# The order of one DMA queue: rows, factors and tiles issued ahead of transfers that wait

## The chip, the cores and the metric

The kernel runs on one core of a Trainium2 chip. The metric is the device time of one execution in microseconds; before the change it is 4508.77 us (median of three runs, 4507.54 to 4514.38). TensorE (PE) multiplies, VectorE (DVE) and ScalarE (ACT) work on elements, and SyncE (SP) issues nearly all DMA transfers, in order, from one queue.

## The reference

Two layers over a batch of 8 entries, N = 2048 nodes, D = 256 channels, H = 8 heads of 32. Cut to what matters:

```python
# layer 0, a graph attention layer; prior is adj too
x_proj = einsum('bnd,hdf->bhnf', x, W)
e = leaky_relu(e_src[..., :, None] + e_dst[..., None, :], 0.2)
e = e + softplus(beta) * log(prior + 1e-6)
attn = softmax(where(adj > 0, e, lowest), axis=-1)
x = layernorm(x + (attn @ x_proj) @ W_out.T)
# layer 1, dot-product attention on the same graph
e = leaky_relu((x @ W1) @ (x @ W2).T, 0.2)
attention = softmax(where(adj > 0, e, -1e12), axis=-1)
x = layernorm(x + relu(attention @ (x @ W3)))
```

Both layers are dense 2048 x 2048 per entry, layer 0 for each of 8 heads.

## The kernel before, in words

Everything is float32. Layer 0 never forms the exponentials of e: with m = the mask times the prior to the power beta, it takes s = max(c, r) * m^T on tiles of 128 source nodes by 2048 target nodes, where c is a row of target factors (the same in all partitions) and r a column of source factors. That is one VectorE instruction (L368), one for each head and tile. The sources' own factor is folded into v (the projected x) and into a column e; both factors come in a small tile `re`, and v in a tile of 2 MB.

A **unit** of layer 0 is a pair of heads `hp` (NP = 4) and a tile `jt` of sources (NT = 16), so 64 units make an entry. `Gat.step` does one: it takes the next m^T tile from `self.mts`, makes two s (L368), loads the next m^T (`mt`, 1 MB, from `mt_d` in HBM), and on TensorE multiplies s with v into `val` and with e into `den` (L403), each product 16 instructions in four column groups. For some jt, listed in `SUMMED`, the den product is left out and s is summed instead in a **chain**: the first jt by ScalarE (`d`, L385), the others by VectorE (L379), and one product with ones at the end of the pair. There are four s tiles (two units), two m^T tiles (tag `mt`), two `d` tiles, three c tiles, and three tiles of tag `ht` that several things share: den's copy `dn`, the reciprocals in rows `rb`, x groups `xg` and the queries h1.

At the end of a pair `finish` copies val and den out, and then works in pieces, one per later unit: it brings den's four rows into a tile of 128 partitions (`rc`, four transfers), takes the reciprocal, stores it in `rec_d`, and, every second pair, loads it back with each row repeated over 32 partitions (`rb`, eight transfers of 128 KB) and multiplies the heads with it (L437).

Layer 1 of an entry (`Dot`) runs beside layer 0 of the next. `Dot.step` does 128 target rows: transposes of p and products with h3 into `acc` (L545, L561), the next rows' scores (`e`, L524; the mask `pen` is loaded here), and z = relu(acc/den) + x1 row (L568, L569; the row is `x1r`, loaded at L566), a layer norm and the store. `fill(k)` puts units of the next entry's layer 0 in three places of the step. Between two entries, at the **turn**, `Gat.output` makes layer 0's end (`y`, L463, with x in groups `xg`), `Gat.turn` the transposes and h3, and `Gat.load` fetches the next entry's v and re.

The projections of all entries, and all of entry 0's layer 0, come first; those of entry 1 stay in SBUF, the others go through `v_d` and `re_d`. TensorE's order is the program's own throughout. From L642 on SyncE's is too: a transfer that waits for its tile holds up everything behind it. Elsewhere, and on VectorE and ScalarE, a scheduler fixes the order when the program is built, from priorities in the program's order and a model of the times.

Of the kernel before, what the change touches and what calls it, by code (L numbers as in the profile page):

```python
# [9 lines left out]
F32 = mybir.dt.float32  # L10
# [8 lines left out]
P = 128  # L19
# [8 lines left out]
def kernel(  # L28
# [26 lines left out]
    nc = tc.nc  # L55
    B, N, D = x.shape
    H, _, DH = w_proj.shape
    NT = N // P
# [3 lines left out]
    HALF = N // 2  # L62
    HP = 2
    NP = H // HP
    IG = BK // P


    SUMMED = [[()] * NP, [(2, 4, 5)] + [(1, 4, 7, 10, 13)] * (NP - 1)]
    SUMMED += [[(2, 4, 5)] + [(1, 3, 5, 7, 9, 11, 13)] * (NP - 1)] * (B - 2)

    const = ctx.enter_context(tc.tile_pool(name="const", bufs=1))
    dram = ctx.enter_context(tc.tile_pool(name="dram", bufs=1, space=DRAM))
# [86 lines left out]
    c_d = dram.tile([B, H, N], F32, name="c_d")  # L159
    v_d = dram.tile([B, P, NT, D], F32, name="v_d")  # L160
    re_d = dram.tile([B, P, 2, NT, H], F32, name="re_d")
    rec_d = dram.tile([B, NP, 4, HALF], F32, name="rec_d")
    x1_d = dram.tile([B, N, D], F32, name="x1_d")

    def load_x(b, g):
# [34 lines left out]
    def load_mt(jt, deep):  # L200
        mt = wide_tile("mt", "d" if deep and jt % 2 else "mt", 2)
        nc.sync.dma_start(mt, mt_d[ts(jt, P), :])
        return mt
# [26 lines left out]
    def row_tile(name, bufs=4):  # L230
        return small.tile([P, D], F32, tag="row", name=name, bufs=bufs)


    class Gat:
# [73 lines left out]
        def load(self):  # L308
            self.v = whole.tile([P, NT, D], F32, name="v")
            nc.sync.dma_start(self.v, v_d[self.b])  # L310
            self.re = small.tile([P, 2, NT, H], F32, name="re", bufs=3)
            nc.sync.dma_start(self.re, re_d[self.b])

# [6 lines left out]
        def load_ahead(self):  # L320


            self.mt_loads = (load_mt(jt, False) for _ in range(self.b, B) for _ in range(NP) for jt in range(NT))
            self.c_loads = (gats[b].query_rows(h) for b in range(self.b, B) for h in range(H))
            self.mts, self.cs_ahead = [], []
            for _ in range(2):
                self.cs_ahead.append(next(self.c_loads))
                self.mts.append(next(self.mt_loads))
            self.cs_ahead.append(next(self.c_loads))

        def follow(self, gat):

# [10 lines left out]
        def step(self, count=1):  # L343

            for _ in range(count):
                hp, jt = next(self.units)
                for work in list(self.later):
                    if next(work, self) is self:
                        self.later.remove(work)
                if jt == 0:  # L350
                    if self.b > 0:
                        self.cs = [self.cs_ahead.pop(0) for _ in range(HP)]
                    else:
                        self.cs = [self.query_rows(hp * HP + a) for a in range(HP)]
                    self.val = pacc.tile([P, HALF], F32, tag="val", name="val")
                    self.den = pacc.tile([P, HALF], F32, tag="den", name="den")
                first = self.b == 0 and hp == 0
                if first:
                    self.more_mt(jt + 2, jt > 0)
                if self.b > 0:  # L360
                    mt = self.mts.pop(0)
                else:
                    mt = self.mts[jt] if first else load_mt(jt, True)
                s = []
                for a in range(HP):
                    h = hp * HP + a
                    sa = wide_tile("s", "s", 4)
                    nc.vector.scalar_tensor_tensor(sa, self.cs[a], self.re[:, 0, jt, h:h + 1], mt, ALU.max, ALU.mult)  # L368
                    s.append(sa)
                    if self.b > 0 and jt == NT - 1:  # L370
                        self.cs_ahead += [c for c in [next(self.c_loads, None)] if c]
                if self.b > 0:
                    self.mts += [t for t in [next(self.mt_loads, None)] if t]
                v, e = self.v, self.re[:, 1]
                heads = [hp * HP + a for a in range(HP)]
                chain = SUMMED[self.b][hp]
                if jt - 1 in chain[1:]:
                    for d, sa, h in zip(self.sums, self.last, heads):
                        nc.vector.scalar_tensor_tensor(d, sa, e[:, jt - 1, h:h + 1], d, ALU.mult, ALU.add)  # L379
                self.last = s  # L380
                self.products(self.val, [v[:, jt, ts(h, DH)] for h in heads], s, jt == 0, jt == NT - 1)
                if jt in chain[:1]:
                    self.sums = [wide_tile("d", "d", 2) for _ in heads]
                    for d, sa, h in zip(self.sums, s, heads):
                        nc.scalar.activation(d, sa, AF.Copy, scale=e[:, jt, h:h + 1])  # L385
                if jt not in chain:
                    self.products(self.den, [e[:, jt, h:h + 1].to_broadcast([P, DH]) for h in heads], s, jt == 0,
                                  not chain and jt == NT - 1)
                if chain and jt == NT - 1:
                    self.products(self.den, [ones] * HP, self.sums, False, True)  # L390
                if jt == NT - 1:
                    work = self.finish(hp)
                    next(work)
                    if self.b == 0:
                        for _ in work:
                            pass
                    else:
                        self.later.append(work)
# [8 lines left out]
        def finish(self, hp):  # L407

            b, lo = self.b, hp % 2 * HP * DH
            if hp == 0:
                self.ht = whole.tile([P, NT, KC, P], F32, tag="heads", name="ht")
            ht = self.ht[:, :, hp // 2, :]
            for s in range(2):
                nc.scalar.copy(ht[lo:lo + HP * DH, ts(s, NT // 2), :],
                               self.val[ts(s, HP * DH), :].rearrange("p (t i) -> p t i", i=P))
            dn = chunk.tile([P, HALF], F32, tag="ht", name="dn", bufs=3)
            nc.scalar.copy(dn, self.den)
            yield  # L420
            yield
            rc = small.tile([P, HALF // DH], F32, name="rc", bufs=1)
            for q in range(4):
                nc.sync.dma_start(rc[ts(q, DH), :], dn[q * DH:q * DH + 1, :])
            nc.vector.reciprocal(rc, rc)
            yield
            nc.sync.dma_start(rec_d[b, hp].rearrange("q (p c) -> (q p) c", c=HALF // DH), rc)
            if lo == 0:
                return
            yield  # L430
            for s in range(2):
                rb = chunk.tile([P, HALF], F32, tag="ht", name="rb", bufs=3)
                for a in range(2 * HP):
                    nc.sync.dma_start(rb[ts(a, DH), :], rec_d[b, hp - 1 + a // HP, s * HP + a % HP:s * HP + a % HP + 1, :]
                                      .to_broadcast([DH, HALF]))
                half = ht[:, ts(s, NT // 2), :]
                nc.vector.tensor_mul(half, half, rb.rearrange("p (t i) -> p t i", i=P))  # L437

# [61 lines left out]
    class Dot:  # L500
# [34 lines left out]
        def step(self, fill=lambda k: None):  # L535


            it, (p, den) = self.at, self.ahead
            self.at += 1
            fill(0)  # L540

            def turned(g):
# [19 lines left out]
            fill(2)  # L562
            rec = small.tile([P, 1], F32, name="rec1", bufs=2)
            nc.vector.reciprocal(rec, den)
            xr = row_tile("x1r")
            nc.sync.dma_start(xr, x1_d[self.b, ts(it, P), :])  # L566
            z = row_tile("z")
            nc.scalar.activation(z, acc, AF.Relu, scale=rec)  # L568
            nc.vector.tensor_add(z, z, xr)  # L569
# [61 lines left out]
    count = (B - 1) * NT  # L631
    for k in range(1, NP * NT + 1):
        g0.step()
        if k % 2 == 0:
            for _ in range(k * count // (NP * NT) - (k - 2) * count // (NP * NT)):
                next(projections)
            if k > NT:
                next(weights, None)
# [5 lines left out]
    for b in range(1, B + 1):  # L644
        gat, fresh = gats[b - 1], gats[b] if b < B else None

        def layer_0(count):
            if fresh:
                fresh.step(count)

        if b == 1:
            fresh.load_ahead()
        elif fresh:
            fresh.load()
            fresh.follow(gat)
        rows, turns = gat.output(), gat.turn()
        if dot is None:
            layer_0(4)
            next(rows)
            next(projections)  # L660
            layer_0(2)
        else:

            dot.step(lambda k: layer_0((0, 2, 2)[k]))
            if not fresh:
                for work in gat.later:
                    for _ in work:
                        pass
            next(rows)
            dot.step(lambda k: layer_0((0, 2, 0)[k]))  # L670

        for g in range(NB + 2):
            if g < NB:
# [43 lines left out]
```

## Time and profile before

| | |
|---|---|
| time, median of three runs | 4508.77 us |
| span of the profiled execution | 4502.4 us |
| TensorE, VectorE, ScalarE busy | 4279.3, 3604.1, 1661.5 us |
| mean granted TensorE clock | 0.980 |
| HBM traffic | 185 GB/s over the span |
| m^T loads | 496 of 1024 KB, median 4.9 us to landing |
| x1r loads | 128 of 128 KB, median 4.8 us to landing |
| rb loads | 128 of 128 KB, median 5.5 us to landing |

In the profile a line such as "L368 DVE" names the kernel's line and the engine. Behind a group stands its busy time, the mean of one in ns, and the engine's idle time just before it with what ended it. In a timeline the columns are start, duration, engine, line, operation, out<-in, count, and in brackets the idle time before it and who ended it. A transfer in SyncE's queue is shown when it is issued, after its waits; when it lands isn't in the row.

### The profile page before, as it was taken

How to read it: one execution, taken by the hardware profiler on the slowest of the kernel's cores; microseconds unless marked ns; L12 is line 12 of the kernel's file. 1: busy time of each engine (PE TensorE's matmuls, PEld its weight loads, DVE VectorE, ACT ScalarE, POOL GpSimd, SP SyncE). 2: the span in 40 equal slices, each digit the busy share in tenths (PEclk: the TensorE clock that was granted, in tenths of full speed). 3: DMA queues.
4: the chain of work that ended last, by engine and by line, in shares of the span. 5: the costliest groups of instructions: out<-in, count | busy, mean ns of one | idle time of the engine just before them, and what ended most of it. 6: DMA issues, size and time to landing. Idle time of an engine off the chain costs nothing.

```text
span 4502.4 us, 59957 instructions
## 1 busy us (share of the span) xinstructions
PE 4279.3 (95%) x25040; PEld 2217.8 (49%) x25040; DVE 3604.1 (80%) x2610; ACT 1661.5 (37%) x3021; POOL 9.5 (0%) x14
## 2 busy tenths in 40 slices
PE   7999799998999999998999989999999989999999
PEld 4444255454544445544455545444454544544666
DVE  6888778887798878888789977988798887899222
ACT  6522133332333323332333323333333323433455
POOL 0000000000000000000000000000000000000000
PEclk9999899999999999999999999999999999999999
DMA  8877555656455564555555464555645455554211
GB/s 255 291 266 264 204 204 212 217 194 228 169 188 184 191 216 144 189 184 196 188 188 181 164 215 167 188 187 188 210 147 195 178 202 186 183 183 143 74 50 40
DMA packets 251984, 839.12 MB, mean 186 GB/s; under 512 B 33344, under 2 KB 151872, under 8 KB 176448
## 3 DMA queue, kind: packets, MB, share of 16 engines
q1 hardware_dynamic: 216384, 801.72, 50.4%
q10 hardware_dynamic: 35328, 33.56, 2.2%
q8 instruction: 196, 3.21, 0.3%
q14 instruction: 76, 0.62, 0.0%
HBM read 761.53 MB, written 73.14 MB: 185 GB/s over the span
## 4 chain that ended last, share of the span: by engine, by line
PE 49%; DVE 23%; issue 11%; DMA 6%; ACT 3%; SPq 0%; DVEq 0%; POOL 0%; ACTq 0%; POOLq 0%
DVE s L368 14%; PE acc L561 13%; PE e L524 11%; PE val L403 11%; PE den L403 6%; DVE d L379 4%; PE pt L545 3%; DMA mt<-mt_d 3%; DVE p L529 3%; PE h3p L494 2%; DMA re<-re_d 1%; PE h1p L514 1%; ACT p L532 1%; PE y L463 1%; DMA adj_r<-in_adj_dram 1%
## 5 line engine op out<-in xcount | busy, mean ns | idle before, releaser
L368 DVE SCALAR_TENSOR_TENSOR s<-c,re,mt 128x2048 f32<-128x2048 f32 x1024 | 2362.7, 2341 | 300.6 <-PE den L403 161.7
L403 PE MATMUL val<-s,v 128*32 128x512 f32 x8192 | 1069.2, 611 | 136.4 <-DVE s L368 136.2
L561 PE MATMUL acc<-h,pts 128*128 128x256 f32 x4096 | 956.4, 381 | 18.9 <-ACT pts L547 18.9
L524 PE MATMUL e<-x1t,h 128*128 128x512 f32 x2048 | 904.8, 594 | 2.5 <-ACT h L516 2.5
L561 PEld LDWEIGHTS acc<-h,pts 128*128 128x128 f32 x4096 | 748.7, 191 | 117.2 <-ACT pts L547 30.7
L403 PE MATMUL den<-s,re 128*32 128x512 f32 x5600 | 709.6, 596 | 0.1
L547 ACT COPY pts<-pt 128x512 f32<-128x512 f32 x512 | 296.4, 582 | 942.4 <-PE pt L545 942.1
L403 PEld LDWEIGHTS val<-s,v 128*32 128x32 f32 x8192 | 247.2, 111 | 786.0 <-issue 516.1
L379 DVE SCALAR_TENSOR_TENSOR d<-s,re,d 128x2048 f32<-128x2048 f32 x268 | 622.8, 2342 | 0.0
L524 PEld LDWEIGHTS e<-x1t,h 128*128 128x128 f32 x2048 | 379.0, 190 | 454.0 <-issue 414.8
L529 DVE CUSTOM_DVE_ANT_0 p<-p,pen 128x2048 f32<-128x2048 f32 x128 | 292.4, 2284 | 229.7 <-ACT p L526 229.4
L526 ACT ACTIVATE p<-e 128x512 f32<-128x512 f32 x512 | 303.9, 594 | 422.8 <-PE e L524 420.9
L403 PEld LDWEIGHTS den<-s,re 128*32 128x32 f32 x5600 | 192.2, 111 | 429.9 <-issue 424.1
L545 PEld LDWEIGHTS pt<-ident,p 128*128 128x128 f32 x2048 | 239.6, 141 | 229.3 <-issue 178.2
L532 ACT ACTIVATE p<-p,neg 128x2048 f32<-128x2048 f32 x128 | 256.7, 2006 | 212.6 <-DVE neg L529 212.6
L545 PE MATMUL pt<-ident,p 128*128 128x128 f32 x2048 | 320.8, 280 | 5.2 <-ACT p L532 5.2
L569 DVE TENSOR_TENSOR z<-z,x1r 128x256 f32<-128x256 f32 x128 | 53.8, 420 | 205.9 <-ACT z L568 97.8
L568 ACT ACTIVATE z<-acc,rec 128x256 f32<-128x256 f32 x128 | 61.0, 476 | 284.5 <-PE acc L561 230.0
L270 PE MATMUL proj<-wp,xt 128*128 128x272 f32 (+1 forms) x512 | 134.1, 404 | 15.0 <-ACT both L274 11.1
L494 PE MATMUL h3p<-w3s,x1t 128*128 128x256 f32 x512 | 125.0, 388 | 14.9 <-ACT x1t L489 13.9
L385 ACT ACTIVATE d<-s,re 128x2048 f32<-128x2048 f32 x56 | 111.9, 2009 | 63.9 <-DVE s L368 63.9
L270 PEld LDWEIGHTS proj<-wp,xt 128*128 128x128 f32 x512 | 93.4, 193 | 56.6 <-issue 21.0
(89 smaller groups left out, 1892.6 us busy)
## 6 DMA issues: line engine op xcount, KB each, us to landing
mt<-mt_d SPq DMA_DIRECT2D x496, 1024.0 KB, 4.9
c<-c_d SPq DMA_DIRECT2D x64, 1024.0 KB, 5.5
pen<-pen_d SPq DMA_DIRECT2D x112, 512.0 KB, 5.6
xg<-in_x_dram SPq DMA_DIRECT2D x60, 512.0 KB, 5.0
adj_t<-in_adj_dram SPq DMA_DIRECT2D x16, 1024.0 KB, 8.1
mt_d<-mt SPq DMA_DIRECT2D x16, 1024.0 KB, 5.7
rb<-rec_d SPq DMA_DIRECT2D x128, 128.0 KB, 5.5
x_d<-ht ACTq DMA_DIRECT2D x32, 512.0 KB, 4.3
```

The source lines that it names most:

```text
L270: nc.tensor.matmul(t[:, 0:cols], xt[:, kc, ts(it % IG, P)], wp[:, kc, 0:cols], start=(kc == 0), stop=(kc == KC - 1))
L368: nc.vector.scalar_tensor_tensor(sa, self.cs[a], self.re[:, 0, jt, h:h + 1], mt, ALU.max, ALU.mult)
L379: nc.vector.scalar_tensor_tensor(d, sa, e[:, jt - 1, h:h + 1], d, ALU.mult, ALU.add)
L403: nc.tensor.matmul(dst[ts(q, DH), ts(c, BK)], weights[q % 2], s[q % 2][:, ds(q // 2 * HALF + c * BK, BK)], start=start, stop=stop)
L494: nc.tensor.matmul(t[:, ts(i, D)], x1t[:, kc, ts(2 * (j - 1) + i, P)], w3s[:, kc, :], start=(kc == 0), stop=(kc == KC - 1))
L524: nc.tensor.matmul(t, self.h1[:, kc, ts(it % IG, P)], self.x1t[:, kc, ts(c, BK)], start=(kc == 0), stop=(kc == KC - 1))
L526: nc.scalar.activation(p[:, ts(c, BK)], t, AF.Prelu, alpha=ALPHA)
L529: nc.vector.tensor_tensor_reduce(p, p, pen, -1.0, FMAX, ALU.add, ALU.min, neg)
L532: nc.scalar.activation(p, p, AF.Exp, bias=neg, scale=-1.0, accum_out=den)
L545: nc.tensor.transpose(t[:, ts(k, P)], p[:, ts(g * IG + k, P)], ident)
L547: nc.scalar.copy(pt, t)
L561: nc.tensor.matmul(acc, now[:, ts(k, P)], self.h3[:, j, :], start=(j == 0), stop=(j == NT - 1))
```

## The change

It reorders what SyncE issues, and joins and drops some work around that:

- x1r is loaded at the head of `Dot.step`, not at its end, behind the units' transfers.
- re of the next entry is loaded by `load_factors` at the first unit of the last pair, 16 units before the turn; `load` fetches v alone.
- The first m^T tiles of entry 1 are requested as entry 0's last unit is written, still under the scheduler's order, four instead of two. In entry 1's first pair odd tiles use the two `d` tiles, so four m^T are held; later two again.
- For the `d` tiles to be free, entry 1's first pair has no chain: `()` in place of `(2, 4, 5)`.
- `rc` comes in one transfer instead of four, and each `rb` in one instead of four, from a `rec_d` laid out so that its four rows follow each other.
- At a turn the first x groups (`next(rows)`) are requested behind two units of the second step, not ahead of it.

```diff
-    SUMMED = [[()] * NP, [(2, 4, 5)] + [(1, 4, 7, 10, 13)] * (NP - 1)]
+    SUMMED = [[()] * NP, [()] + [(1, 4, 7, 10, 13)] * (NP - 1)]
...
-    rec_d = dram.tile([B, NP, 4, HALF], F32, name="rec_d")
+    rec_d = dram.tile([B, NP // 2, 2, 2, 2, HALF], F32, name="rec_d")
...
             nc.sync.dma_start(self.v, v_d[self.b])
+
+        def load_factors(self):
             self.re = small.tile([P, 2, NT, H], F32, name="re", bufs=3)
...
-            self.mt_loads = (load_mt(jt, False) for _ in range(self.b, B) for _ in range(NP) for jt in range(NT))
+            self.mt_loads = (load_mt(jt, b == self.b and hp == 0)
+                             for b in range(self.b, B) for hp in range(NP) for jt in range(NT))
...
-            for _ in range(2):
+            for _ in range(3):
                 self.cs_ahead.append(next(self.c_loads))
                 self.mts.append(next(self.mt_loads))
-            self.cs_ahead.append(next(self.c_loads))
+            self.mts.append(next(self.mt_loads))
...
+                if self.b > 0 and hp == NP - 1 and jt == 0 and self.b + 1 < B:
+                    gats[self.b + 1].load_factors()
...
-                if self.b > 0:
+                if self.b > 0 and len(self.mts) < (4 if not SUMMED[self.b][hp] and jt < NT - 4 else 2):
                     self.mts += [t for t in [next(self.mt_loads, None)] if t]
...
-            for q in range(4):
-                nc.sync.dma_start(rc[ts(q, DH), :], dn[q * DH:q * DH + 1, :])
+            nc.sync.dma_start(rc, dn[::DH, :].rearrange("q (p c) -> q p c", c=HALF // DH))
...
-                for a in range(2 * HP):
-                    nc.sync.dma_start(rb[ts(a, DH), :], rec_d[b, hp - 1 + a // HP, s * HP + a % HP:s * HP + a % HP + 1, :]
-                                      .to_broadcast([DH, HALF]))
+                src = rec_d[b, hp // 2, s]
+                nc.sync.dma_start(rb, bass.AP(tensor=src.tensor, offset=src.offset,
+                                              ap=[[HALF, 2 * HP], [0, DH], [1, HALF]]))
...
             it, (p, den) = self.at, self.ahead
             self.at += 1
+            xr = row_tile("x1r")
+            nc.sync.dma_start(xr, x1_d[self.b, ts(it, P), :])
             fill(0)
...
-            xr = row_tile("x1r")
-            nc.sync.dma_start(xr, x1_d[self.b, ts(it, P), :])
...
         g0.step()
+        if k == NP * NT:
+            gats[1].load_ahead()
...
-        if b == 1:
-            fresh.load_ahead()
-        elif fresh:
+        if b > 1 and fresh:
             fresh.load()
...
-            next(rows)
-            dot.step(lambda k: layer_0((0, 2, 0)[k]))
+            def fill(k):
+                if k == 1:
+                    layer_0(2)
+                    next(rows)
+
+            dot.step(fill)
```

More of the change, by code (lines that the diff above doesn't have):

```diff
@@ L422, in finish @@
             rc = small.tile([P, HALF // DH], F32, name="rc", bufs=1)
-            for q in range(4):
-                nc.sync.dma_start(rc[ts(q, DH), :], dn[q * DH:q * DH + 1, :])
+            nc.sync.dma_start(rc, dn[::DH, :].rearrange("q (p c) -> q p c", c=HALF // DH))
             nc.vector.reciprocal(rc, rc)
             yield
-            nc.sync.dma_start(rec_d[b, hp].rearrange("q (p c) -> (q p) c", c=HALF // DH), rc)
+            for s in range(2):
+                nc.sync.dma_start(rec_d[b, hp // 2, s, hp % 2].rearrange("a (p c) -> (a p) c", c=HALF // DH),
+                                  rc[ts(s, HP * DH), :])
             if lo == 0:
```

## The prediction

> **What bounds the kernel now.** I read the page first, then the busy time by stretches, then the timeline of the worst stretch on three engines. The page:
>
> ```profile
> span 4502.4 us, 59957 instructions
> PE 4279.3 (95%) x25040; PEld 2217.8 (49%) x25040; DVE 3604.1 (80%) x2610; ACT 1661.5 (37%) x3021; POOL 9.5 (0%) x14
> ...
> L368 DVE SCALAR_TENSOR_TENSOR s<-c,re,mt 128x2048 f32<-128x2048 f32 x1024 | 2362.7, 2341 | 300.6 <-PE den L403 161.7
> L403 PE MATMUL val<-s,v 128*32 128x512 f32 x8192 | 1069.2, 611 | 136.4 <-DVE s L368 136.2
> ```
>
> TensorE is the bound on average, and of its 223 us of idle time 136 are waits for VectorE's s. Where these lie is told by the busy time of stretches (columns: stretch, length, then each engine's busy time, clock, DMA share, GB/s):
>
> ```profile
> 497.00:570.00 73.00, 46.78 (x266) 14.31 (x259) 61.95 (x51) 9.11 (x16) 0.00 (x0) 0.81 0.61 213
> 1625.00:2064.00 439.00, 434.11 (x2546) 221.79 (x2534) 385.23 (x264) 162.15 (x281) 0.00 (x0) 1.00 0.51 181
> 2064.00:2149.00 85.00, 70.68 (x412) 33.24 (x414) 64.17 (x55) 23.70 (x43) 0.00 (x0) 0.88 0.60 213
> ```
>
> The middle of an entry is full: TensorE idles 4.9 of 439 us, so nothing that speeds other engines there pays. The turn from one entry to the next is not: 14.3 of 85 us idle, and a clock of 0.88. There are six such turns (idle 14.3 to 15.5 us each) and the start of entry 1 (26.2 us). One turn in the timeline, VectorE, TensorE and SyncE's queue (start, duration, instruction, idle before it and who ended it):
>
> ```profile
> 2073.20 0.42 DVE L569 TENSOR_TENSOR z<-z,x1r 128x256 f32<-128x256 f32 x1 [8.81 <-DMA x1r<-x_d]
> ...
> 2078.65 2.35 DVE L368 SCALAR_TENSOR_TENSOR s<-c,re,mt 128x2048 f32<-128x2048 f32 x1 [4.35 <-DMA re<-re_d]
> 2080.92 2.28 DVE L529 CUSTOM_DVE_ANT_0 p<-p,pen 128x2048 f32<-128x2048 f32 x1
> ...
> 2105.64 4.61 DVE L368 SCALAR_TENSOR_TENSOR s<-c,re,mt 128x2048 f32<-128x2048 f32 x2 [4.41 <-PE val L403]
> ```
> ```profile
> 2081.05 1.91 PE L403 MATMUL val<-s,v 128*32 128x512 f32 x2 [3.94 <-DVE s L368]
> 2085.53 2.78 PE L403 MATMUL val<-s,v 128*32 128x512 f32 x11 [2.56 <-DVE s L368]
> ...
> 2119.36 1.92 PE L403 MATMUL val<-s,v 128*32 128x512 f32 x2 [7.14 <-DVE s L368]
> ```
> ```profile
> 2062.02 2.58 SPq L317 DMA_DIRECT2D c<-c_d  x2
> 2064.70 0.38 SPq L202 DMA_DIRECT2D mt<-mt_d  x1
> 2065.12 0.43 SPq L566 DMA_DIRECT2D x1r<-x_d  x1
> 2066.27 0.32 SPq L310 DMA_DIRECT2D v<-v_d  x1
> 2066.64 0.58 SPq L312 DMA_DIRECT2D re<-re_d  x1
> 2067.26 0.44 SPq L209 DMA_DIRECT2D pen<-pen_d  x1
> ```
>
> The reader is to see: the x1 row and the factors re are issued last, behind two c, one m^T and the 2 MB of v. VectorE waits 8.81 us for the row and 4.35 us for the factors, TensorE then waits for s.
>
> Entry 1 starts otherwise: VectorE stands still for 7.99 us until 512.33, waiting for an m^T that SyncE issued at 503.00, behind a 2 MB v_d store (502.14).
>
> [...] SyncE's three xg, which wait for ht tiles, span 13.93 us from 2103.51, and the next m^T goes out at 2117.49, right after the last. [...] 0.50 from 2081 to 2091, with 7.39 us busy, so 3.7 us of work lost.
>
> **The change part by part.**
>
> x1r to the head of the step, re sixteen units early. z needs ScalarE's z too, which ends at 2071.6 (it follows two copies of val and one of den). So z's wait shrinks by only 1.6 us, to 7.2, but with re present VectorE can fill it: m^T and c of the first unit landed by 2066.6, and two of the four s tiles are free then. Static order is the scheduler's, and not known. If two s go ahead of z, VectorE has all four s of units 0 and 1 by 2077.4, then waits for pen (it landed at 2079.82; some 0.4 us earlier without x1r and re in front, still behind v) and does p until 2081.7. TensorE starts val at about 2078 (v, issued at 2066.27, lands some 12 us later) instead of 2081.05, runs units 0 and 1 (4 products of 1.72 us: 6.9) to 2084.9, its transposes and acc (8.4 us, 2095.2 to 2103.6 now) to 2093.3 and the next val to 2095.1, where s tiles come free for unit 4. Now that is 2105.64: 10.5 us earlier, the 3.7 us of half clock included. If the order stays s, p, s, s, s, p still waits for pen until 2079.4 and the gain is 3.5 us. I take 8.5: the first order, less 1 us for semaphores and less 1 us for row sums (below). The 7.14 us before 2119.36 stays: from unit 4's start VectorE needs 13.7 us for two s, two ht products, two d and one s, while TensorE has 2.4 us of work. Six turns: 51 us.
>
> Entry 1: four m^T tiles ahead. m^T 2 and 3 are loaded before the v_d store, as the d tiles are free. The 7.99 us go, and the waits of 0.31 and 2.37 us later: 10.7. Without the chain VectorE drops four d of 2.33 us: 9.3. TensorE gains three den products and drops one against ones, 3 x 1.72 - 1.72 = 3.4 us, beside VectorE, which bounds until 568 (61.95 of 73 us busy against 46.78). TensorE's own work from there, 33.7 us from 506.7, would end at 540.4, before VectorE's 548.5, so VectorE stays the bound and the sum holds: 10.7 + 9.3 = 20.0; the dropped product against ones (1.9 us at 612.4) lies where TensorE is the bound: 1.9. Together about 21.5.
>
> Row sums in single transfers. Four rc issues (2.41 us of SyncE) become one; eight rb (4.99 us) become two. Saved issue time hides nothing now, since SyncE waits for s anyway: 0. On four engines an rb of 512 KB puts 131 KB on each. [...] From above: m^T, 1024 KB, lands in 4.9 us and the fastest x1r, 128 KB, in 2.0, so 896 KB take 2.9 us, 19.3 GB/s per engine, 6.8 us. [...] In the middle of an entry the two ht products come 11.9 and 18.3 us after the first issue (1308.29 to 1320.14 and 1326.59): hidden, but for up to 1 us. In a turn m^T of unit 5 lands behind them, 0 to 1.4 us late: I charge 1.
>
> x groups behind the steps: an m^T now stuck until 2117.49 still lands in time (s of its unit at 2126.7), and the xg, needed at 2137.3, would be issued about 10 us before need with 5 us to land: 0. Waits added for SyncE: x1r's tile was freed two steps earlier and the factors' tile an entry earlier, so nothing is held up. x1r waits in mid-entry (9.2 us of VectorE in 1625 to 2064) go, but TensorE is full there: 0.
>
> Sum: 4508.8 - 51 - 21.5 = 4436.
>
> **Rivals.** (a) The scheduler leaves p in front of s, or pen behind v holds the turn: 6 x 3.5 + 21.5 = 42, so 4466. For it: pen lands 1.1 us before p now. Against: without the wait for re nothing asks for that order. (b) More: the ht products move into the wait before unit 4 and the 7.14 us go too: 6 x 16 + 21.5 = 117, so 4391. Against: their row sums land too late for that. (c) Slower: row sums on four engines become the wait. At 9.2 us later, and 2.9 for m^T behind them, unhidden in six turns (73 us), and 4 us in seven middles (28), 101 is lost against 72.5 gained: 4537. For it: m^T has two tiles only and lands behind. Against: 12 to 18 us of room in the middles.
>
> **How the numbers follow.** Forecast and its neighbourhood (turns worth 6 to 11 us) 0.55, (a) 0.22, (b) 0.12, (c) in full or in part 0.11. The range leaves out half of (b)'s far end and most of (c): 4398 to 4494. Faster by over 0.2% takes the first three, less a little of (a), and the mild part of (c): 0.87; same 0.04; slower 0.09.
>
> **What would show it.** Right: z's wait at a turn is for ScalarE and no longer for x1r; none for re; val after the e products idles about 1 us, not 3.94; clock near 1.00 there; the 7.14 us still present; at entry 1 no 15.20 us gap and some 20 us less to the first h3p. Wrong: VectorE or TensorE waiting for rb, pen or m^T at the turns; rb landing over 15 us after issue and s waiting behind it; TensorE idle in the middles over 10 us.

## The result and the profile after

The changed kernel takes 4540.76 us (median of four runs, 4537.86 to 4541.70) against 4510.67 us for the kernel before, run beside it (four runs, 4507.54 to 4514.38). The ratio is 1.0065, with a 95% interval of 1.0048 to 1.0083: slower by some 30 us, where 73 us of gain had been forecast.

The page of the changed kernel: span, busy time by engine, the chain by line, and four groups (line, engine, operation, tiles, count, then busy time, mean of one in ns, and the engine's idle time ahead of the group with what ended most of it):

```profile
span 4539.9 us, 59623 instructions
...
PE 4289.9 (94%) x25072; PEld 2221.2 (49%) x25072; DVE 3602.1 (79%) x2606; ACT 1660.3 (37%) x3019; POOL 9.5 (0%) x14
...
DVE s L373 13%; PE e L530 12%; PE acc L569 12%; PE val L408 9%; PE den L408 6%; DMA rb<-rec_d 5%; DMA mt<-mt_d 4%; DVE d L384 3%; PE pt L553 3%; PE h1p L520 2%; PE h3p L500 2%; DVE p L535 1%; PE y L469 1%; ACT d L390 1%; ACT p L538 1%
...
L373 DVE SCALAR_TENSOR_TENSOR s<-c,re,mt 128x2048 f32<-128x2048 f32 x1024 | 2354.6, 2342 | 205.7 <-PE den L408 147.1
L408 PE MATMUL val<-s,v 128*32 128x512 f32 x8192 | 1064.0, 613 | 136.6 <-DVE s L373 134.6
...
L575 DVE TENSOR_TENSOR z<-z,x1r 128x256 f32<-128x256 f32 x128 | 54.0, 422 | 164.5 <-ACT z L574 164.3
L443 DVE TENSOR_TENSOR ht<-ht,rb 128x1024 f32<-128x1024 f32 x32 | 39.2, 1225 | 155.2 <-DMA rb<-rec_d 155.2
```

Three things are to be seen. VectorE's s waits 95 us less (205.7, was 300.6), and z waits only for ScalarE's z, no longer for x1r: the reordering did what it was for. TensorE, though, waits for s as long as before (134.6 us, was 136.2). And there is a wait that was not there: VectorE stands 155.2 us, 32 times out of 32, for the row sums `rb`. The 5% of the chain that "DMA rb<-rec_d" holds is the same thing. In the kernel before, that group had no idle time at all.

The same three stretches as before, shifted to the changed kernel's times (start of entry 1, a middle, a turn):

```profile
497.00:570.00 73.00, 60.33 (x385) 22.43 (x383) 62.99 (x57) 8.36 (x25) 0.36 (x1) 0.88 0.71 246
1629.00:2067.00 438.00, 428.88 (x2494) 217.28 (x2487) 378.19 (x262) 159.35 (x277) 0.00 (x0) 1.00 0.50 180
2067.00:2160.00 93.00, 80.52 (x476) 40.46 (x473) 73.73 (x58) 26.72 (x48) 0.00 (x0) 0.91 0.63 220
```

The middle was full, with TensorE idle for 4.9 of 439 us; now it is idle for 9.1 of 438. The turn, in a window of 93 us, still has 12.5 us of idle time (before: 14.3 in 85). The timeline of that turn shows where. VectorE:

```profile
2081.98 0.41 DVE L575 TENSOR_TENSOR z<-z,x1r 128x256 f32<-128x256 f32 x1
...
2099.31 6.78 DVE L373 SCALAR_TENSOR_TENSOR s<-c,re,mt 128x2048 f32<-128x2048 f32 x3
2106.00 0.16 DVE L572 RECIPROCAL rec<-den 128x1 f32<-128x1 f32 x1
2115.72 1.23 DVE L443 TENSOR_TENSOR ht<-ht,rb 128x1024 f32<-128x1024 f32 x1 [9.55 <-DMA rb<-rec_d]
2116.86 0.42 DVE L575 TENSOR_TENSOR z<-z,x1r 128x256 f32<-128x256 f32 x1
2117.19 2.35 DVE L373 SCALAR_TENSOR_TENSOR s<-c,re,mt 128x2048 f32<-128x2048 f32 x1
2120.74 1.23 DVE L443 TENSOR_TENSOR ht<-ht,rb 128x1024 f32<-128x1024 f32 x1 [1.20 <-DMA rb<-rec_d]
```

TensorE, and SyncE's queue:

```profile
2085.51 7.03 PE L530 MATMUL e<-x1t,h 128*128 128x512 f32 x16
2092.47 1.92 PE L408 MATMUL val<-s,v 128*32 128x512 f32 x16
...
2119.59 1.92 PE L408 MATMUL val<-s,v 128*32 128x512 f32 x2 [5.80 <-DVE s L373]
2124.61 4.24 PE L408 MATMUL val<-s,v 128*32 128x512 f32 x16 [3.10 <-DVE s L373]
```
```profile
2101.59 0.33 SPq L202 DMA_DIRECT2D mt<-mt_d  x1
2102.01 1.24 SPq L440 DMA_DIRECT2D rb<-rec_d  x2
```

Up to 2106 the turn is as wanted: z has no wait left, and val follows the e products at once (2092.47; in the kernel before it stood 3.94 us there). Then the ht product stands ahead of unit 4's s in VectorE's order. Before, two s of unit 4 came first (2105.64) and the ht products after them. The kernel before, VectorE and SyncE's queue:

```profile
2110.17 1.22 DVE L437 TENSOR_TENSOR ht<-ht,rb 128x1024 f32<-128x1024 f32 x1
...
2115.83 1.22 DVE L437 TENSOR_TENSOR ht<-ht,rb 128x1024 f32<-128x1024 f32 x1
```
```profile
2097.10 4.99 SPq L434 DMA_DIRECT2D rb<-rec_d  x8
```

So the first product asked for its `rb` 13.1 us after the first issue before; now it asks after 4.2 us (2115.72 less the wait of 9.55, and 2102.01). VectorE must take `rb` first, and that landed 13.7 us after its issue; the s at 2117.19 and TensorE's val at 2119.59 are late with it. The 4.24 us for sixteen val, against 1.92 us at 2092.47, is a second price of this wait: TensorE's granted clock was 0.51 from 2124 to 2129, and 1.00 from 2092 to 2094.4.

In the middle of an entry the same thing happens once per entry, and smaller, except in entry 1, where the waits are 9.54 and 4.31 us (the changed kernel, SyncE's queue and VectorE):

```profile
1842.02 1.23 SPq L440 DMA_DIRECT2D rb<-rec_d  x2
```
```profile
1853.11 1.22 DVE L443 TENSOR_TENSOR ht<-ht,rb 128x1024 f32<-128x1024 f32 x1 [3.73 <-DMA rb<-rec_d]
1858.12 1.22 DVE L443 TENSOR_TENSOR ht<-ht,rb 128x1024 f32<-128x1024 f32 x1 [3.78 <-DMA rb<-rec_d]
```

The first of the two transfers was issued at 1842.02, so its product now asks 7.4 us after the issue (1853.11 less the wait of 3.73), and the second 12.3 us after. The prediction had read 11.9 and 18.3 us from the kernel before, where nothing waited:

```profile
1320.14 1.22 DVE L437 TENSOR_TENSOR ht<-ht,rb 128x1024 f32<-128x1024 f32 x1
...
1326.59 1.22 DVE L437 TENSOR_TENSOR ht<-ht,rb 128x1024 f32<-128x1024 f32 x1
```

Of the 155.2 us, 68 lie in the six turns, 60 in the seven middles, and 27 in entry 0, at the start of entry 1 and at the end.

How many of the core's 16 DMA engines carry an `rb` is estimated here from the trace's packet records, by the packets under way at a time, one to an engine, as the 16 or 17 of the kernel before suggest: the two transfers of a turn have 256 packets of 4096 bytes, and no other transfer has packets of that size in these stretches. In the turn shown, and in the kernel before at its turn:

```
                 first to last packet us   packets under way, most of the time   mean ns of one
before           2100.95 to 2105.46 (4.5)  16 or 17 (3.5 of 4.5 us)              264
changed kernel   2105.99 to 2120.15 (14.2) 4 (11.9 of 14.2 us)                   222 (median 166)
```

### The profile page after: what moved, and what is told of

Read it like the earlier page. It is cut to its first block, busy times and chain, and to the rows that moved or that the text cites. A ratio compares the mean times of both kernels' runs of the same rounds, so it can differ in the third digit from the quotient of the medians.

```text
span 4539.9 us, 59623 instructions
## 1 busy us (share of the span) xinstructions
PE 4289.9 (94%) x25072; PEld 2221.2 (49%) x25072; DVE 3602.1 (79%) x2606; ACT 1660.3 (37%) x3019; POOL 9.5 (0%) x14
## 4 chain that ended last, share of the span: by engine, by line
PE 47%; DVE 20%; DMA 10%; issue 8%; ACT 3%; SPq 0%; DVEq 0%; ACTq 0%
DVE s L373 13%; PE e L530 12%; PE acc L569 12%; PE val L408 9%; PE den L408 6%; DMA rb<-rec_d 5%; DMA mt<-mt_d 4%; DVE d L384 3%; PE pt L553 3%; PE h1p L520 2%; PE h3p L500 2%; DVE p L535 1%; PE y L469 1%; ACT d L390 1%; ACT p L538 1%
## 5 line engine op out<-in xcount | busy, mean ns | idle before, releaser
L373 DVE SCALAR_TENSOR_TENSOR s<-c,re,mt 128x2048 f32<-128x2048 f32 x1024 | 2354.6, 2342 | 205.7 <-PE den L408 147.1
L408 PE MATMUL val<-s,v 128*32 128x512 f32 x8192 | 1064.0, 613 | 136.6 <-DVE s L373 134.6
L443 DVE TENSOR_TENSOR ht<-ht,rb 128x1024 f32<-128x1024 f32 x32 | 39.2, 1225 | 155.2 <-DMA rb<-rec_d 155.2
L500 PE MATMUL h3p<-w3s,x1t 128*128 128x256 f32 x512 | 123.3, 384 | 14.2 <-ACT x1t L495 13.7
L224 ACT ACTIVATE f<-mv,eps_ln 128x1 f32<-128x1 f32 x128 | 37.8, 295 | 250.1 <-DVE mv L222 250.0
```

The source lines that it names most:

```text
L408: nc.tensor.matmul(dst[ts(q, DH), ts(c, BK)], weights[q % 2], s[q % 2][:, ds(q // 2 * HALF + c * BK, BK)], start=start, stop=stop)
L500: nc.tensor.matmul(t[:, ts(i, D)], x1t[:, kc, ts(2 * (j - 1) + i, P)], w3s[:, kc, :], start=(kc == 0), stop=(kc == KC - 1))
```

## The experiments

Two theories at the start. **A**: a single `rb` transfer runs on four engines and lands late, and VectorE's order puts the ht products where it must wait for that. **B**: the reordering of SyncE's transfers itself costs elsewhere. C and D are narrower rivals to A. Times are medians, and ratios are against the kernel before, run beside it on the same chip.

**1. The changed kernel with `rb` in eight transfers again.**

```diff
-                src = rec_d[b, hp // 2, s]
-                nc.sync.dma_start(rb, bass.AP(tensor=src.tensor, offset=src.offset,
-                                              ap=[[HALF, 2 * HP], [0, DH], [1, HALF]]))
+                for a in range(2 * HP):
+                    nc.sync.dma_start(rb[ts(a, DH), :], rec_d[b, hp // 2, s, a // HP, a % HP:a % HP + 1, :]
+                                      .to_broadcast([DH, HALF]))
```

> The changed kernel with one part undone: the reciprocal row sums of a half are read back in eight transfers of 128 KB instead of one of 512 KB; the reordering of SyncE's transfers and the rest stay. Theory A (the single transfer is carried by 4 of 16 DMA engines, lands 13.7 and 18.5 us after its issue, and VectorE's order now has the ht products ahead of unit 4's s, so VectorE and then TensorE stand): the last packets end 8 to 10 us after the issue again, VectorE's 155 us of waits for rb fall under 20, and the time falls by the roughly 10 to 12 us of each of six turns and 8 us of each of seven middles: 4395 to 4440 us. Theory B (the reordering itself costs: early x1r and factors push m^T, c or x groups back): 4500 us or more, since the reordering is still there.

Measured: 4400.03 us, ratio 0.9750 (0.9735 to 0.9764). From 4540.76, that is 140.7 us back for three lines. The page:

```profile
span 4397.3 us, 59797 instructions
...
PE 4238.3 (96%) x25072; PEld 2216.4 (50%) x25072; DVE 3603.7 (82%) x2606; ACT 1665.0 (38%) x3019; POOL 9.7 (0%) x14
...
L408 PE MATMUL val<-s,v 128*32 128x512 f32 x8192 | 1029.7, 602 | 75.1 <-DVE s L373 73.4
```

VectorE does not wait for `rb` once, and TensorE's waits for s fall by 61 us. The two spans differ by 142.6 us: TensorE idles 91.0 us less (159.0 against 250.0) and is busy 51.6 us less (4238.3 against 4289.9) for the same 25072 matmuls. Over a third of what the wait cost was matmuls at a lower clock: the mean granted clock is 0.978 in the changed kernel and 0.989 here. The turn in this kernel, VectorE and TensorE:

```profile
2045.88 4.62 DVE L373 SCALAR_TENSOR_TENSOR s<-c,re,mt 128x2048 f32<-128x2048 f32 x2 [0.26 <-PE val L408]
2050.42 1.22 DVE L443 TENSOR_TENSOR ht<-ht,rb 128x1024 f32<-128x1024 f32 x1
2051.55 4.61 DVE L384 SCALAR_TENSOR_TENSOR d<-s,re,d 128x2048 f32<-128x2048 f32 x2
2056.07 1.22 DVE L443 TENSOR_TENSOR ht<-ht,rb 128x1024 f32<-128x1024 f32 x1
2057.21 9.13 DVE L373 SCALAR_TENSOR_TENSOR s<-c,re,mt 128x2048 f32<-128x2048 f32 x4
```
```profile
2059.61 1.91 PE L408 MATMUL val<-s,v 128*32 128x512 f32 x2 [7.14 <-DVE s L373]
```

The ht products stand behind unit 4's s again, though no line about VectorE was touched: the order on an engine was fixed when the kernel was built, and it came out differently for one transfer than for four. So this run undoes two things at once, the landing time and the place in VectorE's order. The m^T loads behind `rb` add no wait of their own: VectorE waits 43.3 us for m^T in the changed kernel and 42.8 here. Theory B falls: with the whole reordering still in, the kernel is 2.5% faster than before.

**2. A single transfer, but from 16 source rows.** Each reciprocal row is stored four times over.

```diff
+                    for r in range(4):
+                        nc.sync.dma_start(row[r].rearrange("(p c) -> p c", c=HALF // DH), rc[ts(q, DH), :])
...
-                                              ap=[[HALF, 2 * HP], [0, DH], [1, HALF]]))
+                                              ap=[[HALF, 16], [0, P // 16], [1, HALF]]))
```

> The changed kernel, still with a single transfer of 512 KB for each half's row sums, but each reciprocal row is stored four times over, so that the transfer has 16 source rows instead of 4. Theory A (it is the number of engines that counts): packets on all 16 engines, rb landed 8 to 10 us after its issue, VectorE's waits for rb under 40 us, time 4400 to 4450 us. Theory C (a single transfer that is broadcast from DRAM lands late as such, or a single semaphore does): waits for rb as in the changed kernel, 4530 to 4550 us.

Measured: 4438.62 us, ratio 0.9836 (0.9822 to 0.9851). The waits around tile rb in this kernel:

```profile
its engine sat idle before it (us, times) until:
  DMA rb<-rec_d: 15.7, 13
```

From 155.2 us to 15.7, with a transfer that is as single as in the changed kernel. In a turn its 4096-byte packets ran mostly 16 or 17 at a time and took 4.7 us (2059.85 to 2064.56), against 14.2. C falls.

VectorE's order moved here too, to a place between the other two. In that turn, one s of unit 4, both products, then the other s:

```profile
2061.07 2.35 DVE L373 SCALAR_TENSOR_TENSOR s<-c,re,mt 128x2048 f32<-128x2048 f32 x1 [2.15 <-DMA mt<-mt_d]
2063.34 1.22 DVE L446 TENSOR_TENSOR ht<-ht,rb 128x1024 f32<-128x1024 f32 x1
2065.36 1.23 DVE L446 TENSOR_TENSOR ht<-ht,rb 128x1024 f32<-128x1024 f32 x1 [0.80 <-DMA rb<-rec_d]
2066.50 6.87 DVE L373 SCALAR_TENSOR_TENSOR s<-c,re,mt 128x2048 f32<-128x2048 f32 x3
```

But products that ask at the same moment can be compared. In the turns and middles of this kernel the first product asks 7.0 to 8.3 us after the issue and waits 1.35 us at most, in ten of thirteen not at all. In six of the seven middles of the changed kernel it asks 7.3 to 7.4 us after the issue and waits 3.0 to 4.9 us. So the landing time, and with it the number of packets under way (16 or 17 here, 4 in the changed kernel), is a cause of its own, as theory A has it.

The 38 us to experiment 1 were not taken apart. One part is in the trace: the sixteen small stores hold SyncE from 2048.51 to 2055.79 in that turn, and an m^T and both `rb` wait behind them. VectorE's waits for m^T are 72.0 us in this kernel, from 42.8 in experiment 1.

**3. The kernel before with the single `rb` alone** (the same source pattern put into it, and the two stores that the layout needs).

> The kernel before with one part of the change alone: the row sums of a half are read back in one transfer of 512 KB (with the layout and the two stores that this needs). Nothing else is moved. Theory A: VectorE waits for rb as in the changed kernel (100 to 170 us in all) and the time rises by 60 to 130 us, to 4570 to 4640 us. Theory B (the reordering costs, the row sums are hidden): within 10 us of the kernel before, no wait for rb.

Measured: 4638.69 us, ratio 1.0284 (1.0262 to 1.0306): 126 us slower from this part alone. The page:

```profile
L403 PE MATMUL val<-s,v 128*32 128x512 f32 x8192 | 1098.1, 618 | 210.7 <-DVE s L368 210.7
...
L439 DVE TENSOR_TENSOR ht<-ht,rb 128x1024 f32<-128x1024 f32 x32 | 39.2, 1225 | 169.3 <-DMA rb<-rec_d 169.3
```

In a turn of this kernel, with the first `rb` issued at 2156.58:

```profile
2171.73 1.23 DVE L439 TENSOR_TENSOR ht<-ht,rb 128x1024 f32<-128x1024 f32 x1 [11.03 <-DMA rb<-rec_d]
2172.88 2.35 DVE L368 SCALAR_TENSOR_TENSOR s<-c,re,mt 128x2048 f32<-128x2048 f32 x1
```

The first product asks 4.1 us after the issue, instead of 13.1, and stands ahead of unit 4's s: the change of the row sums' transfers alone moves it. The cost is there without any of the reordering, and of about the same size from either side: 126 us added here, 140.7 taken away in experiment 1.

**4. Four engines kept, the ht products asked for one and two units later.**

```diff
+                rbs.append(rb)
+            for s, rb in enumerate(rbs):
+                yield
```

> The changed kernel with the single transfers on four engines kept, but the two ht products asked for one and two units after their loads instead of at once. In VectorE's order only the second of each turn moves, by about one s pair; those of the middles stay a unit's half later than before. Theory A (place in VectorE's order and landing time together make the wait): a partial gain, waits for rb 80 to 140 us instead of 155, time 4500 to 4535 us. Theory D (the waits for rb are only where VectorE would stand anyway, since TensorE sets the pace): no change, 4535 to 4546 us.

Measured: 4508.97 us, ratio 0.9991 (0.9982 to 1.0000); waits for `rb` 111.8 us. A gain of 32 us with the transfers as slow as ever, so the place in VectorE's order is a cause of its own, and D falls. The middles have the larger part in the shorter waits: in six of the seven the first product asks 9.6 us after the issue, instead of 7.3 to 7.4, and the waits for `rb` of all middles fall from 60 us to 33; those of the turns fall from 68 to 54. The gain is partial because the first product of a turn (at 2103.52 in one turn) still stood ahead of unit 4's s, with 8.41 us of wait; the second one, behind both s, no longer waits in five of the six turns. Experiments 2 and 4 show that landing time and place each count. How many of the 140.7 us belong to which stays open: no run has sixteen packets under way and the changed kernel's places in the turn, or four and all the old places.

**5. The kernel before with x1r and the factors ahead, nothing else.**

```diff
             self.at += 1
+            xr = row_tile("x1r")
+            nc.sync.dma_start(xr, x1_d[self.b, ts(it, P), :])
             fill(0)
...
+                if self.b > 0 and hp == NP - 1 and jt == 0 and self.b + 1 < B:
+                    gats[self.b + 1].load_factors()
```

> The kernel before with one part of the change alone: the x1 row is asked for at the head of its step and the factors re in the last pair of the entry before; all else stays, the row sums in eight transfers too. Forecast as recorded: 8.5 us (6 to 11) for each of six turns, so 4512 - 51 = 4461 us (4446 to 4476). From the traces since then (the first s of a turn comes 14 to 15 us earlier, 2 to 8 us of which are given back by unit 4): 4425 to 4447 us. If the reordering costs elsewhere: 4490 us or more.

Measured: 4432.67 us, ratio 0.9827 (0.9813 to 0.9840): 78.4 us, or 13.1 for each of six turns if all of it lies there. In one turn val follows the e products after 0.61 us:

```profile
2064.21 1.92 PE L407 MATMUL val<-s,v 128*32 128x512 f32 x16 [0.61 <-DMA v<-v_d]
2095.29 1.91 PE L407 MATMUL val<-s,v 128*32 128x512 f32 x2 [7.14 <-DVE s L372]
```

**6 to 8. The other parts, each put back as before in the kernel of experiment 1.** The start of entry 1: its first pair sums by the chain again, `SUMMED[1][0] = (2, 4, 5)`, and `load_ahead` is as it was.

> The changed kernel with row sums in eight transfers again, and in addition the start of entry 1 as before: chain in its first pair, two m^T and three c ahead, loaded after entry 0's last step. Against the same kernel with the new start (4400 us): forecast 21.5 us slower, 4415 to 4428 us. Rival: what the chain took from VectorE is hidden behind TensorE, then 4400 to 4408 us.

Measured: 4424.90 us, ratio 0.9812 (0.9799 to 0.9826), so the new start is worth 24.9 us (28 by the difference of the two ratios). Next, `rc` in four transfers and one store (the change has one transfer and two stores):

> The changed kernel with all of the row sums' transfers as before: eight transfers for rb, four for rc and one store. Against eight for rb alone undone (4400 us): forecast 0, since SyncE waits for s tiles anyway: 4394 to 4406 us. Rival (SyncE's issue time counts, 1.9 us more for each pair's four rc): 4407 to 4450 us.

Measured: 4405.10 us, ratio 0.9763 (0.9750 to 0.9776), whose interval overlaps that of experiment 1. Last, `next(rows)` ahead of the second step:

> The changed kernel with row sums in eight transfers again, and in addition the first x group back ahead of the second step, as before. Forecast: 0, 4394 to 4406 us. Rival (xg's wait for its tile blocks m^T behind it on SyncE at each turn): up to 3 us a turn, 4407 to 4420 us.

Measured: 4398.26 us, ratio 0.9749 (0.9735 to 0.9762). Neither of the last two parts can be told from nothing.

**9 and 10. Can the 7.14 us that are left in each turn go?** In the kernel of experiment 1 the first pair of entries 2 to 7 gets another chain:

```diff
-    SUMMED += [[(2, 4, 5)] + [(1, 3, 5, 7, 9, 11, 13)] * (NP - 1)] * (B - 2)
+    SUMMED += [[(6, 8, 10)] + [(1, 3, 5, 7, 9, 11, 13)] * (NP - 1)] * (B - 2)
```

> The changed kernel with row sums in eight transfers again, and the chain d of the first pair of entries 2 to 7 moved from units 2, 4, 5 to units 6, 8, 10, out of the turn: VectorE drops four d of 2.33 us ahead of unit 4's s and makes them later, where it has slack; TensorE's work is the same. If VectorE's work sets the 7.14 us that TensorE stands in each turn: up to 4.7 us of it go in six turns, 4372 to 4390 us. Rival (what stands ahead of s in the turn is waits for m^T and pen, not VectorE's work): 4396 to 4405 us.

Measured: 4395.53 us, ratio 0.9740 (0.9727 to 0.9753): a miss, and not to be told from experiment 1. Busy time by stretches (an 80 us turn and the 65 us after it), first the kernel of experiment 1, then this one:

```profile
1995.00:2075.00 80.00, 72.51 (x443) 36.66 (x442) 71.68 (x46) 25.52 (x41) 0.00 (x0) 0.94 0.68 245
2075.00:2140.00 65.00, 64.14 (x466) 32.73 (x468) 54.90 (x65) 18.81 (x42) 0.00 (x0) 1.00 0.60 218
```
```profile
1992.00:2072.00 80.00, 77.92 (x501) 39.70 (x499) 67.28 (x49) 27.39 (x47) 0.00 (x0) 1.00 0.71 258
2072.00:2137.00 65.00, 60.76 (x413) 30.95 (x412) 60.72 (x62) 17.45 (x37) 0.00 (x0) 0.97 0.57 200
```

In the turn TensorE's idle time falls from 7.5 us to 2.1 and the clock rises to 1.00, as expected. In the stretch after it, where VectorE has the output rows' work, it rises from 0.9 to 4.2, of which 3.6 are waits for s, and the clock falls to 0.97. The slack that was assumed there is not enough for the chain. So with no chain in that pair (`SUMMED` begins with `()` there; the deeper loading of m^T stays for entry 1 alone):

> The same kernel, with no chain at all in the first pair of entries 2 to 7: VectorE drops all six d and ScalarE two, TensorE gains three den products and drops one, 3.4 us net in each of six entries. If VectorE's work sets the wait in the turn: the same gain as with the late chain (about 4.7 us a turn), of which 3.4 is given back: 4385 to 4397 us. Rival (TensorE bounds the pair as a whole): 4400 to 4420 us.

Measured: 4385.11 us (4383.38 to 4387.49), ratio 0.9718 (0.9705 to 0.9732), at the lower edge of what was expected and the best of all kernels run (128 us below the kernel before, which took 4513.26 beside it). TensorE's waits for s are 38.7 us, from 73.4:

```profile
L408 PE MATMUL val<-s,v 128*32 128x512 f32 x8192 | 1022.7, 599 | 41.1 <-DVE s L373 38.7
```

## Why the prediction was wrong

**The step that failed** is "In the middle of an entry the two ht products come 11.9 and 18.3 us after the first issue (1308.29 to 1320.14 and 1326.59): hidden, but for up to 1 us. In a turn m^T of unit 5 lands behind them, 0 to 1.4 us late: I charge 1." It put the row sums at about 6 us in all; experiment 1 measured 140.7. The landing time behind that step was right. Its four engines were an assumption of the author's that no trace of before shows; the packet records of the changed kernel bear it out, with 4 packets under way for 11.9 of 14.2 us, where before 16 or 17 were. For the second transfer this gives 18.5 us at the most, where 9.3 were measured before, an estimate from landings before the change: 2.0 for the fastest x1r, 2.9 for the m^T ahead, and two `rb` of 6.8. It came 18.1 us after its own issue in the turn shown, and over the six turns its product started 18.5 to 21.7 us after the first issue. What failed is the other side of the comparison. The moments at which the products ask for `rb` were read from the kernel before and taken as fixed. They were places in an order that the change also moves: in the middle the first product now asks 7.4 us after the issue instead of 11.9, and in a turn 4.2 us after it instead of 13.1, ahead of unit 4's s instead of behind both. It is the row sums' own transfers that moved them: with these alone in the kernel before (experiment 3) the products move ahead, and with these alone undone (experiment 1) they ask after 11.8 us in a middle and 12.5 in a turn. Why the scheduler places them so was not looked into. Against the old moments the measured landings (11.1 and 16.1 us after the first issue in the middle, 13.7 and 18.7 in the turn, both as shown) would have been hidden or within 1 us of it, as the step says. In the last turn, where the product had asked after 11.5 us and the landings came 14.8 and 21.7 us after the issue, some 4.5 us would have been left, an estimate from these moments. The m^T that the step charges for added no wait. The text itself says of VectorE's s and p that the "static order is the scheduler's, and not known", and did not ask the same of the ht products.

**x1r and re ahead** did what was described: z's wait for x1r and the stop ahead of val are gone, and all four s of units 0 and 1 now stand ahead of p, one ahead of z and three behind it. The size was off: 13.1 us a turn instead of 8.5. In five of the six turns the stretch from the start of the e products to the end of the 7.14 us wait is 48.6 to 49.6 us long in the kernel before and 38.7 to 39.5 in experiment 5: 9.1 to 10.8 us less, which is the 10.5 of the first order, from which 2 us had been taken for caution. The rest came behind that wait, where the prediction put nothing, and was not traced further.

**"The 7.14 us before 2119.36 stays"** was exact in experiments 1 and 5; in the changed kernel's turn 5.80 and 3.10 us stand in its place. One figure of its working is off: from unit 4's start to 2119.36 TensorE had some 6.6 us of work, not 2.4, as 13.7 us less the 7.14 of idle time leave. Experiments 9 and 10 support its reason, VectorE's list of s, products and d: with the d moved or dropped, TensorE's waits for s in the turn are two of 0.86 and 1.22 us.

**Entry 1:** 21.5 us forecast, 24.9 measured.

**x groups and rc at nothing:** measured within the error of nothing.

**The sum.** 78.4 and 24.9 us are 103.3 of the 112.5 us that experiment 1 gains on the kernel before; the 9 us left were not traced to a part. The 140.7 us of the row sums turn that gain into the loss; that is experiment 1 told from its other side, not a second proof. Rival (c), "row sums on four engines become the wait", is what came, and its 4537 us lies close to 4540.76, but through two errors that cancel: it lost 101 where 140.7 was lost, and gained 72.5 where 112.5 was gained. Its 101 us are waits alone, and the idle time measured is close to that, 91.0 us. What it lacked is the clock: after the waits of the turn shown the granted clock was 0.51 and sixteen val took 4.24 us, ahead of them it was 1.00 and they took 1.92 (the 0.50 from 2081 to 2091, with which the prediction works, is the granted clock after a wait of 3.94 us in the kernel before), and 51.6 of the 142.6 us between the two spans were matmuls that ran slower, not idle time.

## What to carry to other kernels

Fewer DMA issues were not cheaper here: in the turns measured, the merged transfers from 4 source rows had mostly 4 packets under way, where eight transfers had 16 or 17; single ones from 16 source rows (experiment 2) had 16 or 17 too. So before merging transfers, count in the packet records how many packets of the merged one run at a time. When a change touches a transfer's size or count, do not take the consumer's place from the old trace; its place in a static order can move with it (here from 13.1 us after the issue to 4.2), and slack read from the old order is not slack that the new one has. A part that is worth nothing by itself (SyncE's issue time: it waits for s anyway, 1731.9 us with the m^T loads alone in the kernel before) should be left out of a change that is worth something: with `rb` in eight transfers this one gains 2.5%.

## What the runs showed of the hardware that was not expected

With four packets under way instead of sixteen the row sums did not take four times as long. The packets of 1 MB of row sums took 4.5 to 4.6 us in two turns of the kernel before, with mostly sixteen under way; with four it took 11.5 to 11.6 us in three middles of the changed kernel and 14.1 to 17.3 in five of its turns, 2.5 to 3.8 times as long. One of these 4096-byte packets took 264 to 270 ns in the mean with sixteen under way, and with four 170 to 176 ns in those middles and 216 to 258 in those turns. What makes the turns slower was not looked into. And the waits that VectorE handed on to TensorE cost more than their length: between the changed kernel and experiment 1, 91.0 us of idle time came with 51.6 us of slower matmuls, at a mean granted clock of 0.978 against 0.989.
